# Layer 0 of a two-layer graph network: VectorE's one-hots of a counted quad are made one step ahead of TensorE's products of them

## The chip, the cores and the metric

The kernel runs on one core of a Trainium2 chip. The metric is the device time of one execution in microseconds (us), as the median of several runs. A profile of one execution gives the durations; its own time stands beside its span in the table below.

## The reference

3125 nodes with 128 features, 100,000 edges sorted by destination, two layers. Layer 0, with which this change deals, is a mean over neighbours, a linear map, an ELU and a layer norm:

```python
    msgs = x[edge_src]
    summed = jax.ops.segment_sum(msgs, edge_dst, num_segments=n_nodes)
    deg = jax.ops.segment_sum(jnp.ones_like(edge_dst, dtype=x.dtype), edge_dst, num_segments=n_nodes)
    mean_neigh = summed / jnp.maximum(deg, 1.0)[:, None]
    return jax.nn.elu(mean_neigh @ W + b)
    ...
    x = _layernorm(x + _L0_gnn_ref(x, src, dst, L0_gnn_W, L0_gnn_b), axis=-1)
    x = _layernorm(x + _L1_gnn_ref(x, edge_index, edge_attr_16, edge_type_4, ...), axis=-1)
```

Layer 1 is a relational attention with 4 relations and 4 heads over the same edges, a feed-forward part and layer norms. It gathers its rows from tables that layer 0's end writes to memory.

## The kernel before

**Tiles.** The edges lie in 784 tiles of 128; four tiles are a quad, so there are 196 quads. Because the edges are sorted, and their destinations crowd at the low nodes, the first 72 quads (`UD`) touch only few destinations each. The sums of layer 0 come about in two ways.

*Gathered quads* (72 to 195). GpSimd fetches the source rows of each tile with one indirect DMA (`gather`, L768), 24 tiles ahead. `sums0` (L1148) multiplies the rows with a one-hot of the destinations (4 tiles, one PSUM tile `sg`) and issues the gathers for the rows that come free. A step later ScalarE copies `sg` to SBUF (`out_copy`, L1158, `sgs`), VectorE makes another one-hot (`spread0`, L1162), and `out0` (L1166) issues six filler products into a part of PSUM that nobody reads (`fo<-ic,il`) and then the two products that spread the sums over 64 nodes (`fo<-ohq,sgs`). `add0` (L1176) adds `fo`, which has one buffer, to the accumulator on VectorE, at a place whose number is loaded into a register.

*Counted quads* (0 to 71). No row is fetched. `count` (L1197) makes for each of the quad's four tiles two one-hots in bf16 on VectorE: `ol` for the low seven bits of the source node, and `oc` for its block of 128 together with the destination. The product of the two, summed over the four tiles in the PSUM tile `dn`, counts how often each source meets each destination. `count_add` (L1209) adds these counts to the matrix `A` on VectorE, again at a loaded place. `ol` and `oc` have four buffers each, `dn` has one. The counted quads come in two segments, quads 0 to 51 and 52 to 71; at the end of each, `counted_sums` (L1223) multiplies `A` with the 25 blocks of `x` and adds the result to the accumulator. `dn` serves for this too.

**The steps.** A loop (L1360) over steps s handles the gathered quad 72 + s, and hangs other work onto it by a table `jobs`: a table of steps and kinds of work. Counted quads are put at steps 3 to 41 and 57 to 71, four to each three steps, so that 36 steps have one and 18 have two. Other jobs are the transposes and linear products of the edge attributes (`edges`, each fourth gathered quad of them all), the turning of attribute chunks, and the 25 node blocks: mean, norm, and a burst of table products (`tables`, L1313) whose results are cut into halves on VectorE a step later (`half`, L1328).

**What sets the order.** `Ordered` (L637) chains the instructions of TensorE, VectorE, ScalarE and SyncE in layer 0 in the order in which the Python code issues them, with no wait; GpSimd has such a chain for its gathers. So the order of the lines in the loop is the order on each engine: on TensorE transposes, the scatter of the last step's quad, linear products, counts, other jobs, row sums, burst; on VectorE halves, destination one-hot, spread one-hot, count one-hots, scatter's add, count's add, other jobs. In a step with two counted quads, the second quad's one-hots stand behind the first one's `count_add`:

```python
                for i, v in enumerate(counts):
                    count(v)
                    if i == 0 and UD < u <= NQ:
                        add0(u - 1)
                    count_add(v)
```

Of the kernel before, what the change touches and what calls it, by code (L numbers as in the profile page):

```python
# [9 lines left out]
F32 = mybir.dt.float32  # L10
I32 = mybir.dt.int32
U16 = mybir.dt.uint16
BF16 = mybir.dt.bfloat16
AF = mybir.ActivationFunctionType
OP = mybir.AluOpType
# [5 lines left out]
P = 128  # L21
N = 3125
E = 100000
F = 128
# [603 lines left out]
NQ = TT // 4  # L628
# [37 lines left out]
UD, ND, SHI = 72, 240, NB2  # L666
# [3 lines left out]
def counted(u):  # L670

    return 8 if u < 24 else 12 if u < SEG[0][1] else 16
# [20 lines left out]
def windows(ctx: ExitStack, tc: tile.TileContext, a, out, flag):  # L693
# [44 lines left out]
    def node(t, eng):  # L738
        return nc.values_load(d0_i[0:1, t:t + 1], engines=[eng], min_val=0, max_val=N - 1,
                              skip_runtime_bounds_check_because="a node's number")  # L740
# [16 lines left out]
    with tc.tile_pool(name="l0c", bufs=1) as l0c:  # L757
        acc0 = l0c.tile([P, 2, NPW], F32, name="acc0")

        XG, TD = 24, 4 * UD  # L760
# [3 lines left out]
        ic = l0c.tile([P, 16 * SHI], BF16, name="ic")  # L764
# [119 lines left out]
        with tc.tile_pool(name="m0c", bufs=1) as m0c, tc.tile_pool(name="l0", bufs=2) as l0, \  # L884
# [3 lines left out]
            pe, ve, act, sp = (Ordered(tc, e) for e in (nc.tensor, nc.vector, nc.scalar, nc.sync))  # L888
# [3 lines left out]
            def at_step(s, eng, f):  # L892
                jobs.setdefault((s, eng), []).append(f)
# [188 lines left out]
            def turned_at(f):  # L1082
                return 6 + f * (NS - 11) // (NQ // 4)
# [30 lines left out]
            X = {}  # L1114

            def onehot4(u):
                o = X["oh", u] = l0.tile([P, 4, WA], F32, name="oh", bufs=3)
                ve.tensor_tensor(o, loc_e[:, 4 * u:4 * u + 4].unsqueeze(2).to_broadcast([P, 4, WA]),
                                 iw[:, :WA].unsqueeze(1).to_broadcast([P, 4, WA]), op=OP.is_equal)
# [38 lines left out]
            def out_copy(u):  # L1158
                g = X["sgs", u] = l0.tile([P, F + 1], F32, name="sgs")
                act.activation(g, X.pop(("sg", u)), AF.Copy)  # L1160
# [5 lines left out]
            def out0(u):  # L1166
                g, q = X.pop(("sgs", u)), X.pop(("ohq", u))

                fb_ = l0p.tile([P, HC], F32, name="fo")
                for _ in range(6):  # L1170
                    pe.matmul(fb_[:, 2 * WQ:2 * WQ + 12 * SHI], il, ic[:, :12 * SHI], start=True, stop=True)
                fo = X["fo", u] = fb_[:, :2 * WQ].rearrange("p (a b) -> p a b", a=2)
                pe.matmul(fo[:, 0], g[:, :F], q, start=True, stop=True)
                pe.matmul(fo[:, 1], g[:, F:].to_broadcast([P, P]), q, start=True, stop=True)

            def add0(u):  # L1176
                n = node(4 * u, ENG.DVE)
                ve.tensor_tensor(acc0[:, :, ds(n, WQ)], acc0[:, :, ds(n, WQ)], X.pop(("fo", u)), op=OP.add)


            A = l0e.tile([P, SHI, ND + 16], F32, name="A")
            lo_f = l0e.tile([P, TD], F32, name="lo_f")
            c_f = l0e.tile([P, TD], F32, name="c_f")
            tmp_i = l0e.tile([P, TD], I32, name="tmp_i")

            def count_columns():
                ve.memset(A, 0.0)
                ve.tensor_scalar(tmp_i, src_e[:, :TD], P - 1, None, op0=OP.bitwise_and)
                ve.tensor_copy(lo_f, tmp_i)
                ve.tensor_scalar(tmp_i, src_e[:, :TD], 7, None, op0=OP.logical_shift_right)  # L1190
                ve.tensor_copy(c_f, tmp_i)
                for u0, u1 in ((0, 24), (24, SEG[0][1]), SEG[1]):
                    c = c_f[:, 4 * u0:4 * u1]
                    ve.tensor_scalar(c, c, float(counted(u0)), -200.0, op0=OP.mult, op1=OP.add)
                ve.tensor_add(c_f, c_f, loc_e[:, :TD])

            def count(u):  # L1197
                w = counted(u)
                cn = l0p.tile([P, SHI, w], F32, name="dn")
                for i in range(4):  # L1200
                    t = 4 * u + i
                    ol = l0.tile([P, P], BF16, name="ol", bufs=4)
                    ve.tensor_scalar(ol, il, lo_f[:, t:t + 1], None, op0=OP.is_equal)
                    oc = l0.tile([P, SHI * w], BF16, name="oc", bufs=4)
                    ve.tensor_scalar(oc, ic[:, :SHI * w], c_f[:, t:t + 1], None, op0=OP.is_equal)
                    pe.matmul(cn.rearrange("p a b -> p (a b)"), ol, oc, start=(i == 0), stop=(i == 3))
                X["cn", u] = cn

            def count_add(u):  # L1209
                n = nc.values_load(dc_i[0:1, u:u + 1], engines=[ENG.DVE], min_val=0, max_val=ND - 1,  # L1210
                                   skip_runtime_bounds_check_because="a node's number, bounded")
                v = A[:, :, ds(n, counted(u))]
                ve.tensor_tensor(v, v, X.pop(("cn", u)), op=OP.add)

            def x_block(b, s):
                n = min(P, N - b * P)
                xb = m0.tile([P, F], F32, name="xb", bufs=7)
                if n < P:
                    ve.memset(xb, 0.0)
                sp.dma_start(xb[:n], a["x"][b * P:b * P + n, :])  # L1220
                return xb

            def counted_sums(g, k):  # L1223
                if k == 0:
                    X["dn"] = l0p.tile([P, 2, ND], F32, name="dn")
                pe.matmul(X["dn"][:, 0], X.pop(("xc", k)), A[:, k, :ND], start=(k == 0), stop=False,
                          skip_group_check=True)
                if k == SHI - 2:
                    X["as"] = l0e.tile([P, ND], F32, name="as")
                    ve.tensor_reduce(X["as"], A[:, :, :ND].rearrange("p s n -> p n s"), AX.X, OP.add)  # L1230
                if k == SHI - 1:
                    pe.matmul(X["dn"][:, 1], ones, X.pop("as"), start=False, stop=True, skip_group_check=True)
                    n = 0 if g == 0 else nc.values_load(
                        dc_i[0:1, UD:], engines=[ENG.DVE], min_val=0, max_val=NP - ND,
                        skip_runtime_bounds_check_because="a node's number, bounded")
                    v = acc0[:, :, ds(n, ND)] if g else acc0[:, :, :ND]
                    ve.tensor_tensor(v, v, X.pop("dn"), op=OP.add)
# [118 lines left out]
            for f in range(NQ // 4):  # L1356
                at_step(turned_at(f), "edges", range(4 * f, 4 * f + 4))
            last = max(s for s, _ in jobs)
            onehot4(UD)
            for s in range(last + 1):  # L1360
                u = UD + s
                for f in jobs.pop((s, "sp"), []):
                    f()
                if UD < u <= NQ:
                    out_copy(u - 1)
                edges = jobs.pop((s, "edges"), [])
                for us in edges:
                    turned(us)
                halves_ = jobs.pop((s, "half"), [])
                if halves_:  # L1370
                    halves_.pop(0)()
                if u + 1 < NQ:
                    onehot4(u + 1)
                if halves_:
                    halves_.pop(0)()
                if u < NQ:
                    spread0(u)
                for f in halves_:
                    f()
                if UD < u <= NQ:  # L1380
                    out0(u - 1)
                for us in edges:
                    lin(us)
                counts = jobs.pop((s, "count"), [])
                for i, v in enumerate(counts):
                    count(v)
                    if i == 0 and UD < u <= NQ:
                        add0(u - 1)
                    count_add(v)
                if UD < u <= NQ and not counts:  # L1390
                    add0(u - 1)
                for us in edges:
                    lin_add(us)
                for e in ("act", "ve"):
                    for f in jobs.pop((s, e), []):
                        f()
                if u < NQ:
                    sums0(u)
                for f in jobs.pop((s, "burst"), []):
                    f()  # L1400
                for us in edges:
                    keep(us)
# [5 lines left out]
    with tc.tile_pool(name="ac", bufs=1) as ac, tc.tile_pool(name="at", bufs=2) as at, \  # L1408
# [93 lines left out]
        for j, (w, x, y) in enumerate((  # L1502
                (W, rF[0:1], rL[0:1]), (WQ - WW + 1, rF4[:, :, 0], rF4[:, :, 3]),
                (WW, rF4[:, :UQ, 0], rL4[:, :UQ, 3]), (WW, rF[0:1, 4 * UQ:4 * UP:2], rL[0:1, 4 * UQ + 1:4 * UP:2]))):
            n = x.shape[1]
# [3 lines left out]
        for u0, u1, j in ((0, 24, 8), (24, SEG[0][1], 9)):  # L1509
# [6 lines left out]
                                op0=OP.subtract, op1=OP.is_gt)  # L1516
# [30 lines left out]
        pe, ve, act, pool, sp = (Ordered(tc, e) for e in (nc.tensor, nc.vector, nc.scalar, nc.gpsimd, nc.sync))  # L1547
# [270 lines left out]
        for s in range(-2, NQ + LATE + 2):  # L1818
            u = s - 1
# [37 lines left out]
    with tc.tile_pool(name="fc", bufs=1) as fc, tc.tile_pool(name="fw", bufs=3) as fw, \  # L1857
# [89 lines left out]
        for bs_ in QS:  # L1947
            o = fw.tile([P, 4, F], F32, name="o")
            for i, b in enumerate(bs_):
                if b % 5 < 2:  # L1950
                    nc.scalar.activation(o[:, i], r1[:, b], AF.Identity, bias=nm[:, b:b + 1], scale=rs3[:, b:b + 1])
                else:
                    nc.vector.tensor_scalar(o[:, i], r1[:, b], mv3[:, b, 0:1], rs3[:, b:b + 1],
                                            op0=OP.subtract, op1=OP.mult)
            b = bs_[0]
            n = min(P, N - b * P)
# [27 lines left out]
```

## Time and profile before

| | |
|---|---|
| median of 3 runs | 2873.77 us (2867.88 to 2883.67) |
| profiled execution: its own time / its span | 2875.92 us / 2874.1 us |
| granted TensorE clock, mean of the span | 0.898 |
| busy: TensorE products, VectorE, GpSimd, ScalarE | 84%, 63%, 43%, 32% of the span |
| layer 0's loop | to about 1077 us |
| counted steps, first segment | 52.6 to 359.1 us, 39 steps |
| counted steps, second segment | 489.4 to 630.7 us, 15 steps |

In the profile a row of a group reads: source line (L647 is the line of the helper that issues all ordered instructions), engine, operation, out<-in by the tiles' names, shapes, count | busy us, mean ns of one | idle us of that engine just before them and what ended it. PE is TensorE's products, PEld its weight loads, DVE VectorE, ACT ScalarE, POOL GpSimd, SP SyncE. A row of the timeline has start, length, engine, instruction, and in brackets the idle time before it. A row of the waits reads "who waited <- for whom: us in total, times, longest". "Remote" is a semaphore whose update came from no instruction that the profile can name, and "issue" a wait for which it shows no cause. `dn<-oc,ol` are the counts' products, `A<-A,dn` is `count_add`, `fo<-ic,il` the fillers, `fo<-ohq,sgs` the scatter, `acc<-acc,fo` is `add0`, `sg<-xg,oh` the row sums, `xg` the gathers.

### The profile page before, as it was taken

The numbers are of one execution on the slowest core, as the hardware profiler recorded it, in microseconds if no ns is written. First come the engines' busy times: TensorE is split into PE (matmuls) and PEld (weight loads), VectorE is DVE, ScalarE is ACT, GpSimd is POOL, SyncE is SP. The second block draws the span as 40 slices with busy tenths as digits, with TensorE's granted clock in tenths as the row PEclk, the third lists the DMA queues.
The fourth block names the chain that finished last, engine by engine and source line by source line (L and its number), as shares of the span: only waits on it lengthen the run. The fifth ranks groups of instructions, "written<-read, shape, count | busy, mean of one in ns | idle before, by whom it ended". The sixth has DMA issues, their size and how long they took to land.

```text
span 2874.1 us, 66163 instructions
## 1 busy us (share of the span) xinstructions
PE 2417.7 (84%) x24485; PEld 1858.4 (65%) x24485; DVE 1821.4 (63%) x6395; ACT 908.9 (32%) x1964; POOL 1245.1 (43%) x1294
## 2 busy tenths in 40 slices
PE   3687777877777685699999999999999999999974
PEld 2454454445444443577777777888888888888853
DVE  6655535653544345377777777777777777776656
ACT  0121112212222231244444444444444443333314
POOL 6555443444434413244444444444444444444400
PEclk9757778878888787799999999999999999999977
DMA  4323344444455456466666667777777789999910
GB/s 128 90 73 104 112 137 142 138 125 155 147 186 173 139 197 227 128 210 205 205 205 208 205 205 216 235 236 235 236 235 233 235 241 245 254 243 246 236 53 24
DMA packets 284394, 520.64 MB, mean 181 GB/s; under 512 B 45833, under 2 KB 144820, under 8 KB 283151
## 3 DMA queue, kind: packets, MB, share of 16 engines
q1 hardware_dynamic: 201588, 273.76, 30.7%
q0 software_dynamic: 78592, 239.71, 29.6%
q8 instruction: 194, 3.18, 0.5%
q10 hardware_dynamic: 3880, 2.84, 0.4%
q14 instruction: 140, 1.15, 0.1%
HBM read 412.10 MB, written 104.82 MB: 180 GB/s over the span
## 4 chain that ended last, share of the span: by engine, by line
PE 48%; DVE 8%; issue 3%; DMA 2%; ACT 0%; SPq 0%; DVEq 0%; ACTq 0%
PE z L647 30%; PE ag L647 7%; PE row L647 6%; DVE wo L647 4%; PE e L647 2%; PE sm_p L647 2%; DMA win<-xr_d 1%; DVE f L647 0%; DVE oh L647 0%; DVE ea L647 0%; PE f L1930 0%; PE f L1922 0%; DVE acc L647 0%; DMA xr_d<-xh 0%; DVE fst L1886 0%
## 5 line engine op out<-in xcount | busy, mean ns | idle before, releaser
L647 POOL DMA_INDIRECT xl<-xl_d,src_e x784 | 751.5, 959 | 895.8 <-PE ag L647 391.5
L647 POOL DMA_INDIRECT xg<-in_x_dram,src_e x496 | 489.0, 986 | 542.6 <-PE sg L647 368.5
L647 ACT ACTIVATE relu<-z 128x512 f32<-128x512 f32 x784 | 449.1, 597 | 793.7 <-PE z L647 611.1
L647 PE MATMUL z<-f_ident,xl 128*128 128x128 f32 x3136 | 476.1, 274 | 0.0
L647 PEld LDWEIGHTS z<-f_ident,xl 128*128 128x128 f32 x3136 | 368.7, 141 | 44.3 <-issue 0.6
L647 PE MATMUL z<-ea,weh 128*128 128x512 f32 x784 | 360.9, 460 | 18.4 <-issue 14.1
L647 PE MATMUL z<-oht,win 96*128 96x128 f32 (+2 forms) x1600 | 343.4, 297 | 4.1 <-DMA win<-xr_d 2.2
L647 PEld LDWEIGHTS z<-oht,win 128*128 128x128 f32 (+1 forms) x1600 | 275.4, 190 | 60.6 <-issue 3.2
L647 PE MATMUL z<-ea,wel 128*128 128x512 f32 x784 | 310.1, 395 | 0.1
L647 PE MATMUL row<-relu,attw 128*32 128x128 f32 x6272 | 247.7, 277 | 31.1 <-issue 29.4
L647 PE MATMUL ag<-xl,wo 128*32 128x128 f32 x6272 | 225.6, 279 | 7.5 <-DVE acc L647 4.2
L647 PEld LDWEIGHTS row<-relu,attw 128*32 128x32 f32 x6272 | 172.6, 109 | 85.0 <-issue 84.0
L647 PE MATMUL xp<-cbl,two 128*128 128x512 f32 x200 | 165.4, 827 | 30.5 <-DVE xh L647 13.1
L647 DVE TENSOR_TENSOR acc<-acc,fo 128x128 f32 x124 | 35.3, 285 | 245.0 <-remote 97.9
L647 PEld LDWEIGHTS ag<-xl,wo 128*32 128x32 f32 x6272 | 181.1, 112 | 9.1 <-DVE acc L647 5.1
L647 DVE TENSOR_TENSOR_SCAN m<-rm,row 128x128 f32<-128x128 bf16 x98 | 41.2, 420 | 228.4 <-PE row L647 228.4
L647 PE MATMUL fo<-ic,il 128*128 128x300 bf16 x744 | 153.5, 357 | 37.4 <-DVE acc L647 31.3
L647 DVE CAST xh<-xp 128x512 fp32r<-128x512 f32 x100 | 69.0, 690 | 157.3 <-PE xp L647 113.7
L647 PEld LDWEIGHTS z<-ea,weh 128*128 128x128 f32 x784 | 149.5, 191 | 27.5 <-issue 27.5
L647 ACT ACTIVATE xlr<-xp 128x512 f32<-128x512 f32 x100 | 59.7, 597 | 304.3 <-PE xp L647 156.2
L647 PEld LDWEIGHTS z<-ea,wel 128*128 128x128 f32 x784 | 150.1, 191 | 9.0 <-issue 0.4
L647 DVE SCALAR_TENSOR_TENSOR ea<-far,e 128x512 fp32r<-128x512 bf16 x196 | 132.2, 675 | 36.7 <-remote 35.6
(327 smaller groups left out, 4059.3 us busy)
## 6 DMA issues: line engine op xcount, KB each, us to landing
win<-xr_d SPq DMA_DIRECT2D x224, 256.0 KB
xr_d<-xh SPq DMA_DIRECT2D x100, 512.0 KB
win<-xr_d SPq DMA_DIRECT2D x176, 192.0 KB
xl_d<-xlr SPq DMA_DIRECT2D x100, 258.0 KB
sg<-seg_d SPq DMA_DIRECT2D x196, 128.0 KB
rm<-rq_d SPq DMA_DIRECT2D x98, 128.5 KB
eat_d<-emt SPq DMA_DIRECT2D x196, 64.0 KB
xl<-xl_d,src_e POOLq DMA_INDIRECT x784
```

Of the source, the lines that this page charges most:

```text
L647: ins = f(*args, **kw)
```

## The change

`count` is split. It now only makes the one-hots of a quad and keeps them; `count_out` issues their four products, and `count_add` is as before. `ol` and `oc` get eight buffers each. In the loop, the one-hots made in a step are kept in `made`, and their products come in the next step: the first quad's at its head, ahead of `out_copy` and of the transposes and the scatter; its `count_add` behind the halves and the spread one-hot on VectorE; a second quad's products behind the scatter; the new one-hots behind these; then `add0`; then the second quad's `count_add`. To make room, the integer work tile of `count_columns` becomes a view of `A`, which is cleared after it; `as`, a sum over `A`, takes a buffer of the table rows `xlr`; and the blocks of `x` get six buffers for seven.

```diff
-            tmp_i = l0e.tile([P, TD], I32, name="tmp_i")
+            tmp_i = A.rearrange("p s n -> p (s n)")[:, :TD].bitcast(I32)
...
             def count(u):
-                w = counted(u)
-                cn = l0p.tile([P, SHI, w], F32, name="dn")
+
+                n = SHI * counted(u)
                 for i in range(4):
                     t = 4 * u + i
-                    ol = l0.tile([P, P], BF16, name="ol", bufs=4)
+                    ol = l0.tile([P, P], BF16, name="ol", bufs=8)
                     ve.tensor_scalar(ol, il, lo_f[:, t:t + 1], None, op0=OP.is_equal)
-                    oc = l0.tile([P, SHI * w], BF16, name="oc", bufs=4)
-                    ve.tensor_scalar(oc, ic[:, :SHI * w], c_f[:, t:t + 1], None, op0=OP.is_equal)
+                    oc = l0.tile([P, n], BF16, name="oc", bufs=8)
+                    ve.tensor_scalar(oc, ic[:, :n], c_f[:, t:t + 1], None, op0=OP.is_equal)
+                    X["oc", t] = ol, oc
+
+            def count_out(u):
+                cn = X["cn", u] = l0p.tile([P, SHI, counted(u)], F32, name="dn")
+                for i in range(4):
+                    ol, oc = X.pop(("oc", 4 * u + i))
                     pe.matmul(cn.rearrange("p a b -> p (a b)"), ol, oc, start=(i == 0), stop=(i == 3))
-                X["cn", u] = cn
...
-                xb = m0.tile([P, F], F32, name="xb", bufs=7)
+                xb = m0.tile([P, F], F32, name="xb", bufs=6)
...
-                    X["as"] = l0e.tile([P, ND], F32, name="as")
+                    X["as"] = m0.tile([P, ND], F32, name="xlr", bufs=3)
...
+            made = []
             onehot4(UD)
             for s in range(last + 1):
                 u = UD + s
                 for f in jobs.pop((s, "sp"), []):
                     f()
+                if made:
+                    count_out(made[0])
                 if UD < u <= NQ:
                     out_copy(u - 1)
...
+                for v in made[:1]:
+                    count_add(v)
                 if UD < u <= NQ:
                     out0(u - 1)
+                for v in made[1:]:
+                    count_out(v)
                 for us in edges:
                     lin(us)
                 counts = jobs.pop((s, "count"), [])
-                for i, v in enumerate(counts):
+                for v in counts:
                     count(v)
-                    if i == 0 and UD < u <= NQ:
-                        add0(u - 1)
+                if UD < u <= NQ:
+                    add0(u - 1)
+                for v in made[1:]:
                     count_add(v)
-                if UD < u <= NQ and not counts:
-                    add0(u - 1)
+                made = counts
```

More of the change, by code (lines that the diff above doesn't have):

```diff
@@ L1183, in windows @@
             c_f = l0e.tile([P, TD], F32, name="c_f")
-            tmp_i = l0e.tile([P, TD], I32, name="tmp_i")
+            tmp_i = A.rearrange("p s n -> p (s n)")[:, :TD].bitcast(I32)
             def count_columns():
-                ve.memset(A, 0.0)
                 ve.tensor_scalar(tmp_i, src_e[:, :TD], P - 1, None, op0=OP.bitwise_and)
@@ L1191, in count_columns @@
                 ve.tensor_copy(c_f, tmp_i)
+                ve.memset(A, 0.0)
                 for u0, u1 in ((0, 24), (24, SEG[0][1]), SEG[1]):
```

## The prediction, on record before the result was known

> **What bounds the kernel now.** I first read the page's slices and its chain, then the busy times by stretch, then the groups by shape, the waits, and last the timeline of one step. The chain that ended last begins only with layer 0's last tables (its first long piece is a table product at 1104 us), so it doesn't show what paces the counted steps. They must be judged in their own stretches: 88 to 359 us (quads 0 to 51, after a start held up by weight loads) and 489 to 631 us (quads 52 to 71).
>
> ```profile
> PEclk9757778878888787799999999999999999999977
> ```
> ```profile
> 88.00:359.00 271.00, 211.84 (x1141) 131.71 (x1141) 163.93 (x686) 43.17 (x101) 137.93 (x143) 0.69 0.33 95
> 489.00:631.00 142.00, 112.91 (x563) 65.61 (x562) 90.25 (x322) 31.07 (x76) 54.95 (x57) 0.82 0.42 144
> ```
>
> The columns are stretch, length, busy PE, PEld, DVE, ACT, POOL, granted clock, DMA share, GB/s. TensorE is busy 78% and 80% of the time, VectorE 60% and 64%, nobody is full, and TensorE runs at 0.69 and 0.82 of its clock. Two in-order engines pass work to and fro. Where TensorE loses time to it:
>
> ```profile
> L647 PE MATMUL dn<-oc,ol 128*128 128x300 bf16 x112 | 30.8, 356 | 17.5 <-remote 5.6 <-DVE ol L647 3.3 <-DVE oc L647 3.2
> L647 PE MATMUL dn<-oc,ol 128*128 128x200 bf16 x96 | 24.8, 324 | 14.0 <-DVE oc L647 6.4 <-issue 2.8 <-DVE xlr L647 2.6
> L647 PE MATMUL dn<-oc,ol 128*128 128x400 bf16 x80 | 24.8, 380 | 10.3 <-DVE oc L647 5.3 <-DVE ol L647 2.2 <-issue 1.5
> ```
>
> These are the counts' products; the figure behind the second bar is TensorE's idle time just ahead of them: 17.5 + 14.0 + 10.3 = 41.8 us. One step with two counted quads shows the mechanism, TensorE first, then VectorE:
>
> ```profile
> 132.41 0.51 PE L647 MATMUL dn<-oc,ol 128*128 128x200 bf16 x4
> 134.99 1.35 PE L647 MATMUL dn<-oc,ol 128*128 128x200 bf16 x4 [2.07 <-DVE oc L647]
> 136.27 0.66 PE L647 MATMUL sg<-xg,oh 128*32 128x129 f32 x8
> 136.86 1.68 PE L647 MATMUL fo<-ic,il 128*128 128x300 bf16 x6
> 138.33 0.95 PE L647 MATMUL fo<-ohq,sgs 128*128 128x64 f32 x4
> ```
> ```profile
> 131.72 0.29 DVE L647 TENSOR_TENSOR acc<-acc,fo 128x128 f32 x1 [1.16 <-issue]
> 134.22 0.36 DVE L647 TENSOR_TENSOR A<-A,dn 128x200 f32 x1 [2.22 <-PE dn L647]
> 134.50 0.25 DVE L647 TENSOR_SCALAR ol<-il,lo_f 128x128 bf16<-128x128 bf16 x1
> ```
>
> VectorE had made the first quad's one-hots by 130.6 and then stood, first for the scatter's sum, then for the counts (its add started 1.3 us after the last product's recorded end, 132.92). Only then could it make the second quad's one-hots, and TensorE stood 2.07 us. Gathers aren't the limit: they follow at 1.25 us (218.52, 219.77, 221.03 in GpSimd's timeline), so 5.0 us for a step's four, while 54 counted steps take 448 us from 52.6 to 359.1 and 489.4 to 630.7, 8.3 each. GpSimd waits for TensorE.
>
> ```profile
> POOL xg L647 <- PE sg L647: 92.9, 28, 14.4
> DVE A L647 <- PE dn L647: 25.5, 26, 3.3
> ```
>
> [...] with a grant of 0.50 from 107.0 to 124.1 us[...]: that stretch was busy 16.10 of 17.10 us. [...] the second quad's one-hots, which need no product's result, start behind the waiting add. [...] another such add started 0.42 us after its product. That spread is the main uncertainty below.
>
> **The change, part by part.** The sum is made against the profiled execution's own 2875.92 us (span 2874.1); the median of the runs is 2873.77, 2.1 less.
>
> 1. *The one-hots move a step ahead.* 72 quads keep 8 one-hots, 4 products and one add each; nothing is added to or taken from any engine. A step now begins on TensorE with the first quad's four products, whose one-hots are finished. The second quad's products follow the scatter's products, and by then the first add has freed their bank: behind the first products TensorE has 6 filler and 4 scatter products (1.68 + 0.95, about 2.4 us at half clock), against 0.4 to 1.3 us of hand-over and 0.36 to 0.57 us of add. So the 41.8 us go, but for two terms: 2.5 us lie at 83 us, in the start that waits for weights and can't gain; and the 5.6 us "remote" is a product's semaphore that came late, which may strike elsewhere, so I count half of it. Removed: 41.8 - 2.5 - 2.8 = 36.5 us (bounds 30 and 39.3).
>
> 2. *The clock.* A clock of 0.69 means half speed for (1 - 0.69) / 0.5 = 62% of the stretch; 212 us busy are then 212 / 1.62 = 131 us of full-speed work. If closing the gaps cuts the slow share by a fifth (to 50%), that saves 131 x 0.12 = 16 us; in the second stretch (36% to 29%, 113 / 1.36 = 83 us) another 6. Half of these 22 us will lie beside other waits: 11 us gained. Nothing in the trace shows a step after the change, so the bounds are wide: 35 gained if the slow share nearly halves, 10 lost[...].
>
> 3. *What the moved waits hold up.* On VectorE the first count's add now stands ahead of the next step's one-hots, and the scatter's add behind all of these; the next step's filler products wait for the scatter's add, since `fo` has one buffer. The way from the head's products to that add: hand-over 0.4, add 0.4, four pairs of one-hots 1.5 us (129.05 to 130.56; 3.0 where two quads are made), scatter's add 0.3, hand-over 0.2: 2.8 or 4.3 us. Beside it TensorE has, in a bare step at half clock, filler and scatter 2.4, row sums 0.6, next head 1.1: 4.1 us; at full clock half of it, 2.1. So it is short by 0.2 us in double steps at half clock, by 0.7 and 2.2 us at full clock. With full clock in some 45% of the 54 steps: 36 x 0.45 x 0.7 + 18 x (0.45 x 2.2 + 0.55 x 0.2) = 11 + 20 = 31 us as the upper bound. Transposes, linear products and tables lengthen the cover in many steps, and a bare step at full clock meets the 5.0 us of its gathers anyway; lower bound 0. I take 13 us lost.
>
> 4. *The rest.* `tmp_i` in A's place and the later memset: same instructions at step 1, before the weights hold everything; nothing. `as` in the ring of `xlr`: asked for at steps 54 and 84, whose last table rows left four and more steps before, and freed a step later; nothing. `xb` with 6 for 7 buffers: two are loaded and two used per step on SyncE's queue, a step ahead, so 4 live; nothing, or a wait of SyncE that TensorE doesn't see. GpSimd's queue keeps its order: its gathers come when row sums free their rows, sooner if TensorE is sooner. One step less lies between the last count and the blocks' sums; the add stands ahead of them on VectorE, so about 1 us twice at worst, within the rounding.
>
> Sum: -36.5 - 11 + 13 = -34.5 us: 2875.9 - 34.5 = 2841.4 profiled, less 2.1: **2839 us** as a median. Layer 1 starts when layer 0's last tables are out, by order and not by the clock, so the whole passes through to the end.
>
> **Rivals.** *The stall only moves (0.23).* The scatter's add becomes the late one: all 31 us of step 3, no gain of clock: 2873.8 - 36.5 + 31 = 2868 us. For it speaks "PE fo <- DVE acc", with 6.7 us already waited in the first stretch; against it, that these are 3 waits only, two of them behind late semaphores. *More than I think (0.14).* The clock comes free and step 3 is covered: -39.3 - 35 = -74, 2799 us; for it speaks that half the TensorE time there is at half speed, against it the 16.10 of 17.10 us that didn't release it. *Slower (0.13).* VectorE's early wait for the step's head is the mechanism: a hand-over of 1.3 us as at 134.22, not 0.4, now stands ahead of one-hots and scatter's add in each of the 54 steps. At two thirds of them exposed, 36 x 0.9 = 32 us, with the 31 of step 3 and a clock 5 lost to the idling: 2873.8 - 36.5 + 31 + 32 + 5 = 2905 us. It decides from 36.5 / 54 = 0.7 us per counted step put on TensorE's path. That the change doesn't do what it says is unlikely: buffers for 8 tiles hold just the two quads of a step.
>
> **Chances.** The forecast's own case has 0.50 (about 2820 to 2858). A measurement of this kernel can tell about 0.5%, 14.4 us, from no change. Faster by more: 0.50 + 0.14 = 0.64; within: 0.23; slower: 0.13. The range goes from the best case, 2799, to 2885, the sum of the bad bounds (-30 + 10 + 31 = +11); outside lie most of the slow case and a tail of the fast one.
>
> **What would show it.** Right: idle ahead of `dn<-oc,ol` under 8 us (now 41.8), "DVE A <- PE dn" still there, clock from 88 to the end of the first counts above 0.69, counted steps at about 7.6 us. Step 3 wrong: "PE fo <- DVE acc" above 20 us in counted steps. The prediction is wrong if TensorE's idle time there stays at its 59 + 29 = 88 us in the two stretches under other names, or if time is lost after 631 us, which no step of mine explains.

## The result, and the profile after

The changed kernel takes **2839.97 us** (median of 4 runs, 2831.36 to 2846.67), the kernel before beside it 2870.82: a ratio of 0.9895, 95% interval 0.9856 to 0.9933, or 31 us. The forecast was 2839. The sum came out; its terms didn't, as the profile of the changed kernel shows. Its profiled execution took 2831.36 us (span 2829.6), the shortest of the four.

The page's row of granted clocks, and the stretches that hold the same work before and after. The scatter's sum `acc` serves as a mile post: the counted steps lie between its 5th and 42nd execution, 37 steps, and between its 57th and 72nd, 15 steps. Columns as in the prediction (length, then busy PE, PEld, DVE, ACT, POOL, clock). First the kernel before:

```profile
86.50:368.00 281.50, 216.45 (x1170) 134.84 (x1169) 165.73 (x696) 44.20 (x103) 143.49 (x148) 0.69 0.33 94
498.20:632.40 134.20, 105.32 (x538) 62.09 (x537) 83.88 (x306) 27.36 (x67) 55.91 (x58) 0.81 0.40 134
```

Then the changed one:

```profile
PEclk8677788887788887899999999999999999999967
```
```profile
82.20:354.50 272.30, 191.30 (x1173) 132.31 (x1172) 166.51 (x696) 44.22 (x102) 140.01 (x146) 0.74 0.33 97
489.30:608.90 119.60, 91.42 (x522) 57.66 (x521) 82.05 (x299) 25.93 (x64) 57.92 (x60) 0.87 0.45 146
```

The two stretches together shrink from 415.7 to 391.9 us, 24 us. TensorE's *busy* time falls by 39 us (321.8 to 282.7) with the same products; its *idle* time, which the change was to remove, rises by 15 us (93.9 to 109.2). By the end of layer 0's loop (the start of the last `acc`, 1077.1 and 1045.7 us) the changed kernel is 31 us ahead.

The groups of the counts' products, changed kernel (behind the bar: busy, mean ns, idle just ahead):

```profile
L647 PE MATMUL dn<-oc,ol 128*128 128x300 bf16 x112 | 27.5, 371 | 7.1 <-DVE A L647 3.8 <-PE sg L647 2.2 <-issue 0.5
...
L647 PE MATMUL dn<-oc,ol 128*128 128x400 bf16 x80 | 20.9, 371 | 7.5 <-DVE A L647 2.9 <-PE sg L647 2.6 <-issue 1.1
...
L647 PE MATMUL dn<-oc,ol 128*128 128x200 bf16 x96 | 18.3, 317 | 11.4 <-DVE A L647 6.0 <-issue 3.5 <-DVE ol L647 1.4
```

The idle time here fell from 41.8 to 26.0 us. One-hots are named only once among the first three causes, with 1.4 us; what is named first is `A`, the add that frees the one bank of `dn`. New idle time came up elsewhere. Here is the scatter in the whole program, before and after:

```profile
L647 PE MATMUL fo<-ohq,sgs 128*128 128x64 f32 x496 | 94.5, 326 | 68.3 <-issue 49.2 <-ACT sgs L647 19.1
```
```profile
L647 PE MATMUL fo<-ohq,sgs 128*128 128x64 f32 x496 | 92.1, 320 | 91.0 <-issue 62.7 <-ACT sgs L647 28.3
```

In the two stretches alone it is 10.2 and then 31.9 us, and ahead of `mw<-vt,emt`, products of the edge attributes, 10.1 and then 17.8. Both read what ScalarE copies, though for most of this time the trace names no cause ("issue"). And ScalarE waits like this (waits of the changed kernel: us in total, times, longest):

```profile
ACT sgs L647 <- remote: 152.2, 29, 11.4
...
DVE acc L647 <- remote: 43.8, 8, 11.9
...
DVE A L647 <- remote: 14.0, 5, 5.9
```

One such event, ScalarE first, then TensorE:

```profile
116.60 0.28 ACT L647 ACTIVATE sgs<-sg 128x129 f32<-128x129 f32 x1 [10.03 <-remote]
```
```profile
109.05 0.66 PE L647 MATMUL sg<-xg,oh 128*32 128x129 f32 x8
...
110.67 0.93 PE L647 MATMUL fo<-ic,il 128*128 128x300 bf16 x6
116.93 1.09 PE L647 MATMUL fo<-ohq,sgs 128*128 128x64 f32 x4 [5.33 <-issue]
```

The row sums ended at 109.7 us; ScalarE copied them at 116.6, with nothing else to do, and TensorE stood 5.3 us for the copy. I call a hand-over late if its consumer, being idle, starts over 2 us after the recorded end of the products that it needs. Counted for `acc`, `sgs` and `A`, the kernel before has 42 late ones, 183 us in all, the changed one 52, 235 us. That could be the change's doing or the chip's; runs on other chips are set beside it below.

### The profile page after: what moved, and what is told of

The parts are those of the page before. It is cut to its first block, busy times and chain, and to the rows that moved or that the text cites. A ratio compares the mean times of both kernels' runs of the same rounds, so it can differ in the third digit from the quotient of the medians.

```text
span 2829.6 us, 66188 instructions
## 1 busy us (share of the span) xinstructions
PE 2375.0 (84%) x24485; PEld 1850.4 (65%) x24485; DVE 1822.5 (64%) x6395; ACT 909.4 (32%) x1964; POOL 1240.3 (44%) x1294
## 4 chain that ended last, share of the span: by engine, by line
PE 49%; DVE 8%; issue 3%; DMA 1%; ACT 0%; DVEq 0%; SPq 0%; ACTq 0%
PE z L647 30%; PE ag L647 7%; PE row L647 6%; DVE wo L647 4%; PE e L647 2%; PE sm_p L647 2%; DVE f L647 1%; DMA win<-xr_d 1%; DVE ea L647 0%; DVE oh L647 0%; PE f L1942 0%; PE f L1934 0%; DVE y L647 0%; DVE de L647 0%; DVE m L647 0%
## 5 line engine op out<-in xcount | busy, mean ns | idle before, releaser
L647 PEld LDWEIGHTS z<-f_ident,xl 128*128 128x128 f32 x3136 | 368.1, 141 | 44.3 <-issue 0.6
L647 PE MATMUL fo<-ohq,sgs 128*128 128x64 f32 x496 | 92.1, 320 | 91.0 <-issue 62.7
L647 PE MATMUL fo<-ic,il 128*128 128x300 bf16 x744 | 143.9, 341 | 27.3 <-issue 18.3
L647 PEld LDWEIGHTS fo<-ohq,sgs 128*128 128x128 f32 x496 | 85.5, 240 | 112.3 <-issue 70.9
```

The lines of the kernel that those rows point to most:

```text
L647: ins = f(*args, **kw)
```

## The experiments

Mile posts are used throughout: "stretches" are the two above, with 37 and 15 steps. The first four kernels ran on one chip, where the kernel before took 2868.15 us (40 runs). "The first chip" stands for this one and for the result above, which has the same time before (2870.82) and the same late hand-overs.

**The changed kernel again** (e1)

> The changed kernel once more. If its profile is typical: about 2840 us, ratio 0.989, TensorE's idle time ahead of the counts' products near 20 us (42 before) and some 25 us more than before ahead of the scatter's products, behind ScalarE's copy. If the first profile was a lucky one, layer 1 (from the last scatter's sum to the end), which was 13 us shorter there, comes back to 1797 us as in the kernel before, and the loop of layer 0 keeps its 31 us.

Measured: 2843.29 us, ratio 0.9917 (0.9891 to 0.9944). Stretches 388.0 us, busy 279.5, idle 108.5: the same signs as above, less busy and more idle than before. Idle time ahead of the counts' products is 32.7 us, where I expected near 20; ahead of the scatter's it is 27 us more than before, as expected. The loop ends 25.8 us ahead. Layer 1 took 1794 us, before 1797, and 1784 in the first profile. Those 13 us are no part of the change: e3 below, which gains nothing, has 1784 too.

**The buffers alone** (e2): the kernel before with the room changes and eight buffers, in the old order.

```diff
-                    ol = l0.tile([P, P], BF16, name="ol", bufs=4)
+                    ol = l0.tile([P, P], BF16, name="ol", bufs=8)
```

> The kernel before with all that makes room (work tile in A, the sum in the table rows' ring, six blocks of x) and with eight buffers of each one-hot, but the old order of the step. Theory (what counts is where the one-hots stand in VectorE's order): no gain, 2868 to 2874 us, idle ahead of the counts' products still about 42 us. Rival (buffers or the moved tiles bring it): about 2840 us.

Measured: 2862.87 us, 0.9984 (0.9958 to 1.0009). Buffers and room bring nothing that can be told from zero.

**All one-hots first, in the same step** (e3): two quads' one-hots and the scatter's sum ahead of both quads' products, no step of lead.

```diff
+                for v in counts:
+                    count(v)
+                if UD < u <= NQ:
+                    add0(u - 1)
+                for v in counts:
+                    count_out(v)
+                    count_add(v)
```

> Eight buffers, no lead: in a step all its one-hots are made first, then the scatter's add, then products and add of the first quad, then of the second. So only the round trip in the 18 steps with two quads goes. Theory (the lead counts): half of the gain or less, 2853 to 2865 us, with TensorE still waiting for one-hots of the same step. Rival (only the one-hots behind the add were the stall): the whole gain, about 2840 us.

Measured: 2863.56 us, 0.9995 (0.9977 to 1.0013). Idle time ahead of `dn<-oc,ol` is 50.5 us (20.0 + 12.5 + 18.0), of which 27.4 us are named `A`: the second quad waits for its bank where it waited for one-hots. TensorE's busy time in the stretches falls by 20 us (321.8 to 302.1), and its idle time rises by 17.5 (93.9 to 111.4).

**The lead, with the products in their old place** (e4): one-hots a step ahead, but the products stand behind scatter and linear products, and on VectorE the scatter's sum and the first add stand ahead of the one-hots.

```diff
-                if made:
-                    count_out(made[0])
...
+                for v in made[:1]:
+                    count_out(v)
...
+                for v in made[:1]:
+                    count_add(v)
+                for v in made[1:]:
+                    count_out(v)
+                for v in counts:
+                    count(v)
```

> One-hots a step ahead as in the changed kernel, but the products stay where they were, behind the scatter and the linear products, and on VectorE both adds come ahead of the new one-hots. Theory (the lead counts, not the place at the step's head): within 8 us of the changed kernel, 2832 to 2848 us. Rival (the gain comes from products at the head, which fill TensorE's wait for ScalarE's copy of the row sums): most of it goes, 2855 us or more.

Measured: 2878.74 us, 1.0030 (1.0011 to 1.0049), slower. My theory, that the lead is what counts and its place doesn't, fell here. But this kernel changes two things at once, the place on TensorE and the order on VectorE, so the next two kernels look at each.

The next four ran on a second chip. There the kernel before takes 2552.17 us, 11% less, and in none of these four traces does any hand-over to `acc`, `sgs` or `A` come over 2 us late.

**The sum ahead of the one-hots** (e5): the changed kernel, one thing altered.

```diff
-                for v in counts:
-                    count(v)
                 if UD < u <= NQ:
                     add0(u - 1)
+                for v in counts:
+                    count(v)
```

> The changed kernel with one thing altered: VectorE makes the scatter's sum (acc) ahead of the one-hots of the next step, not behind them; the products keep their new places (first quad at TensorE's head of a step, second behind the scatter's products). Four cells are compared with this one: head/behind (the changed kernel, 2843), head/ahead (this), old place/ahead (2879, measured), old place/behind. If the place of the products carries the gain, this one is 2840 to 2850 us, and a few us faster than the changed kernel if step 3 of the prediction (the scatter's sum held up by the one-hots) is real. If VectorE's order carries it (one-hots ahead of every wait for a product), this one loses most of the gain: 2860 to 2880 us, with idle time ahead of dn<-oc,ol back above 30 us.

**Both products in the old place** (e6): one-hots a step ahead and ahead of the sum, the products behind scatter and linear products, both adds of the counts last on VectorE. So the first add moves too, which it must: its products come later.

```diff
-                if made:
-                    count_out(made[0])
...
-                for v in made[1:]:
+                for v in made:
+                    count_out(v)
                     count_add(v)
```

> The fourth cell: one-hots a step ahead and on VectorE ahead of the scatter's sum, as in the changed kernel, but both counted quads' products stand on TensorE behind the scatter's products and the linear products, as before the change, and VectorE makes both adds of the counts last. If the place at the step's head carries the gain (TensorE has finished work at hand while ScalarE copies the row sums), this one loses it: 2865 to 2885 us, as the run with the old place and the adds first. If VectorE's order carries it, this one keeps it: 2838 to 2850 us.

Measured: e5 2530.06 us, 0.9918 (0.9894 to 0.9942), the ratio that I had expected if the place carries the gain, but with 47.4 us of idle time ahead of the counts' products, which I had expected if VectorE's order does; e6 2572.01 us, 1.0076 (1.0050 to 1.0102). What the four cells mean is told below, with the changed kernel's run on such a chip.

**The scatter a step further behind** (e7, on the changed kernel; e8, on the kernel before): takes away what TensorE waits for when it waits for `sgs` of the same step.

```diff
-                if UD < u <= NQ:
-                    out0(u - 1)
+                if UD + 1 < u <= NQ:
+                    out0(u - 2)
```

> The changed kernel, and the scatter's products and their sum a further step behind (the row sums of quad u are copied by ScalarE in step u+1 as now, and used in step u+2; the last two quads are caught up in one step; three buffers of ohq for two; blocks that are not the last start a step later). TensorE then never waits for the copy sgs of the same step. If the changed kernel's remaining idle time (27.5 us ahead of fo<-ohq,sgs in the first stretch) is ScalarE's wait and its late hand-overs, it is faster than the changed kernel by 10 to 35 us: 2808 to 2833. If that idle time only takes another name (the sum's slot, gathers, the wait for emt), it stays within 2838 to 2850.

> The kernel before with the same lag of the scatter's products, no one-hot ahead. If the old order's loss is the one-hots' own (TensorE stands until they are made), the lag helps both kernels alike or the old one less: 2845 to 2870, and 20 us or more above the changed kernel with the lag. If the changed kernel's gain is that its products fill the time of ScalarE's copy, the lag takes that time away for both, and this one comes within 10 us of the changed kernel with the lag.

Measured: e7 2511.45 us, 0.9841 (0.9813 to 0.9868); e8 2570.46 us, 1.0066 (1.0030 to 1.0102). With the old order the lag gains nothing in the stretches (349.8 us; e12 below has 345.0) and loses behind the last count (338.5 us; e12 has 323.2). The two kernels with the lag are 59 us apart, not within 10. So on this chip the wait for ScalarE's copy isn't what the change is worth. There was little of it to win: on calm chips TensorE's idle time ahead of the scatter's products is 0.4 us in the stretches of the kernel before and none in the changed one. On the first chip, where it is 10.2 and 31.9 us, the lag wasn't tried, so the forecast for e7 wasn't tested where it was made.

The last four ran on a third chip, as calm as the second: 2553.38 us before, no late hand-over.

**The two kernels on a calm chip** (e11 the changed one, e12 the one before)

> The changed kernel once more, beside the kernel before on one chip. The last four kernels ran on a chip on which the kernel before takes 2552 us, not 2870, and on which no product's semaphore came over 2 us late (on the first chip some 190 to 240 us of such late hand-overs per run). If the gain doesn't rest on the late hand-overs, the ratio is 0.990 to 0.994 on either chip (2527 to 2537, or 2842 to 2853). If the change only hides part of them, the ratio is above 0.997 on the calm chip. With the sum ahead of the one-hots at 0.9918, step 3 of the prediction (13 us) would put this one at 0.997.

> The kernel before, for its profile on this chip: the stretch of counted steps (scatter sums 4 to 41) to set beside the others. On the calm chip, 207 us with the place at the head, 237 with the old place and the one-hots a step ahead, 233 with the old order and the lag. If the head's place carries the gain, the kernel before takes 225 to 235 us there, with the clock near 0.76; and idle time ahead of dn<-oc,ol of 30 us or more.

Measured: changed 2504.20 us, ratio **0.9800** (0.9765 to 0.9836), a gain of 49 us where the first chip gave 25 to 31. I expected 0.990 to 0.994 or less of a gain; it is more. So late hand-overs aren't what the change hides. Where they occur the gain is about half as large; which of TensorE's waits make the difference is told further below. The kernel before came out as expected (first stretch 233.2 us at a clock of 0.75, 44.7 us idle ahead of the counts). Before, then changed (stretches, and the counts' groups):

```profile
65.90:299.10 233.20, 196.09 (x1167) 124.35 (x1166) 165.81 (x695) 44.56 (x103) 152.09 (x158) 0.75 0.39 116
395.70:507.50 111.80, 91.90 (x539) 54.82 (x538) 83.75 (x307) 27.47 (x67) 55.01 (x57) 0.92 0.48 160
```
```profile
64.20:256.60 192.40, 162.74 (x1159) 115.48 (x1159) 163.18 (x696) 44.09 (x102) 146.39 (x152) 0.85 0.46 139
353.40:455.60 102.20, 87.59 (x525) 56.43 (x524) 81.27 (x299) 26.48 (x64) 55.24 (x58) 0.92 0.50 168
```
```profile
L647 PE MATMUL dn<-oc,ol 128*128 128x300 bf16 x112 | 29.6, 329 | 14.9 <-DVE oc L647 11.2 <-DVE ol L647 0.7
...
L647 PE MATMUL dn<-oc,ol 128*128 128x200 bf16 x96 | 24.4, 314 | 17.6 <-DVE oc L647 13.6 <-DVE ol L647 2.1 <-DVE acc L647 0.2
L647 PE MATMUL dn<-oc,ol 128*128 128x400 bf16 x80 | 23.9, 364 | 12.2 <-DVE oc L647 10.7
```
```profile
L647 PE MATMUL dn<-oc,ol 128*128 128x300 bf16 x112 | 25.8, 343 | 3.5 <-DVE A L647 1.8 <-DVE ol L647 0.8 <-DVE oc L647 0.2
...
L647 PE MATMUL dn<-oc,ol 128*128 128x400 bf16 x80 | 19.4, 345 | 6.0 <-DVE oc L647 2.8 <-DVE A L647 2.6
...
L647 PE MATMUL dn<-oc,ol 128*128 128x200 bf16 x96 | 15.5, 264 | 10.2 <-DVE oc L647 4.7 <-DVE ol L647 2.2 <-DVE A L647 2.0
```

Here the account is clean. The stretches shrink by 50.4 us (345.0 to 294.6), as much as the whole gain. TensorE's busy time falls by 37.7 (288.0 to 250.3), the same as on the first chip (39.1, and 42.3 in the repeat); its idle time falls by 12.7 (57.0 to 44.3), where it rose by 15 on the first chip. Ahead of the counts 25.0 us of idle time go in the whole program (44.7 to 19.7), 21.7 of them in the stretches (40.9 to 19.2); there 9.8 us come back as the wait for the scatter's sum, "PE fo <- DVE acc" (none before, 6.4 and 3.4 in the two stretches now). In TensorE's account the chips differ in the idle term and hardly in the busy one. VectorE is busy for 244 of the 295 us, 83%, more than before (250 of 345, 72%).

The four cells (products' place, and the scatter's sum against the next step's one-hots on VectorE), with the stretches together; the kernel before has 1 and 345.0 us:

| | one-hots ahead of the sum | sum ahead of the one-hots |
|---|---|---|
| first products at the step's head | 0.9800, 294.6 us (the change) | 0.9918, 320.9 us (e5) |
| products behind scatter and linear products | 1.0076, 364.1 us (e6) | 1.0030 (e4, first chip) |

Three cells are on the two calm chips, whose times before agree to 0.05%; the fourth is on the first chip, so its ratio isn't strictly comparable. The head's place, with the early add that it allows, is needed: without it, neither order that was tried gains. With it, the order on VectorE is worth another 26 us of the stretches. In e6 TensorE waits for the sum and for the bank:

```profile
PE fo L647 <- DVE acc L647: 37.4, 24, 7.6
...
PE dn L647 <- DVE A L647: 33.0, 18, 2.5
```

The same double step in the changed kernel and in e5 shows what VectorE's order does. VectorE of the changed kernel, then of e5:

```profile
139.13 0.34 DVE L647 TENSOR_TENSOR A<-A,dn 128x200 f32 x1
139.41 0.24 DVE L647 TENSOR_SCALAR ol<-il,lo_f 128x128 bf16<-128x128 bf16 x1
...
142.38 0.27 DVE L647 TENSOR_TENSOR acc<-acc,fo 128x128 f32 x1
...
143.96 0.47 DVE L647 TENSOR_TENSOR A<-A,dn 128x300 f32 x1
```
```profile
151.33 0.34 DVE L647 TENSOR_TENSOR A<-A,dn 128x200 f32 x1
151.87 0.29 DVE L647 TENSOR_TENSOR acc<-acc,fo 128x128 f32 x1 [0.20 <-PE fo L647]
152.08 0.25 DVE L647 TENSOR_SCALAR ol<-il,lo_f 128x128 bf16<-128x128 bf16 x1
...
156.66 0.47 DVE L647 TENSOR_TENSOR A<-A,dn 128x300 f32 x1
```

In the changed kernel VectorE makes one-hots while TensorE scatters, and the sum finds its products long done. In e5 it stands 0.20 us for the scatter, the one-hots start later, and the next add, which frees the bank for the second quad, comes 5.33 us after the last one, not 4.83. TensorE then stands 1.57 us ahead of the second quad's products, against 0.46; the changed kernel pays 0.95 us of that back ahead of the fillers, where it waits for the sum. One pair of steps proves little, since the difference goes from -2.5 to +3.5 us over the 52 steps. The counts' groups of e5 show it for all of them:

```profile
L647 PE MATMUL dn<-oc,ol 128*128 128x300 bf16 x112 | 25.9, 320 | 16.1 <-DVE A L647 9.4 <-DVE oc L647 3.0 <-DVE ol L647 1.6
L647 PE MATMUL dn<-oc,ol 128*128 128x400 bf16 x80 | 21.9, 371 | 12.3 <-DVE A L647 6.9 <-DVE oc L647 4.7
L647 PE MATMUL dn<-oc,ol 128*128 128x200 bf16 x96 | 17.7, 278 | 19.0 <-DVE A L647 10.9 <-DVE oc L647 6.0 <-DVE ol L647 0.9
```

The wait for `A` is 27.2 us, against 6.4 in the changed kernel. In the stretches e5 stands 26.3 us longer ahead of the counts' products (45.5 for 19.2) and 9.8 us less for the sum; other idle time adds 5.0 us and busy time 4.8.

**The lag only in the counted steps** (e9): e7 was 20 us slower than e5 behind the last count (339.4 to 319.2), so here the lag ends there, and between the segments.

```diff
+            def late(s):
+                return int(s <= 43 or 58 <= s <= 72)
...
+                todo = [v for v in range(UD, min(u, NQ)) if v > done and v < u - late(s)]
```

> The changed kernel with the scatter's products a further step behind only in the steps with counts (0 to 43 and 58 to 72), caught up in the step after. In the run with the lag everywhere, the counted steps went at 5.0 us (185.1 us for 37, the gathers' pace), 22 us below the run without the lag, but the steps after the last count were 20 us longer (339.4 for 319.2). If the loss there comes of the lag in those steps, this one keeps both: 20 us below the lag everywhere, ratio 0.974 to 0.979. If it comes of the earlier start of the later steps (clock or tables due at the same time), the ratio stays at 0.982 to 0.986.

Measured: 2506.56 us, 0.9794 (0.9755 to 0.9834), the same as the changed kernel, and neither of the two outcomes in full. The later part is indeed as without the lag (319.4 us), but the counted steps did not keep what e7 had there (287.4 us in the stretches): they take 297.9, the changed kernel 294.6. No version that I tried beats the change beyond its interval.

**Fillers in the old gap** (e10): is it the clock?

```diff
+                    if i == 0:
+                        for _ in range(3):
+                            pe.matmul(cn.rearrange("p a b -> p (a b)"), il, ic[:, :SHI * w], start=True, stop=True)
```

> The kernel before with three filler products (il by ic, of the counts' own size, into the counts' bank, overwritten by the counts) ahead of each quad's products, where TensorE stands until the one-hots are made; nothing computed is altered. If the gain of the change is mostly TensorE's clock[...], this one gains too: ratio 0.990 to 0.997, with the clock in the counted steps up by 0.08 or more. If the gain is the products' own place (work at hand in ScalarE's time), the fillers only delay: ratio 0.999 to 1.008.

Measured: 2541.38 us, 0.9949 (0.9928 to 0.9970), faster by 12 us. The stretches:

```profile
65.90:288.80 222.90, 190.01 (x1312) 126.61 (x1311) 166.21 (x698) 44.51 (x103) 150.84 (x157) 0.87 0.41 120
383.70:498.10 114.40, 98.31 (x599) 59.00 (x598) 83.71 (x306) 27.45 (x67) 54.16 (x56) 0.97 0.46 155
```

216 useless products, 41.4 us busy (16.0 + 13.4 + 12.0 in their groups), lie in TensorE's queue, and the program is faster: the clock rises from 0.75 to 0.87 and from 0.92 to 0.97, and TensorE's busy time, fillers included, stays at 288.3 us (288.0 without), so all other products took some 41 us less. The stretches shrink by 7.7 us, all of it idle time (57.0 to 49.0). So the clock is a lever by itself. The change gets less clock and more gain: it pays for no fillers, and its products need 250.3 us.

## Why the prediction was right in sum and wrong in its terms

| step, in the stretches | predicted | calm chip | first chip |
|---|---|---|---|
| 1, idle ahead of the counts | -36.5 | -21.7 | -18.1 |
| 2, TensorE's busy time (clock) | -11 | -37.7 | -39.1 |
| 3, idle ahead of the fillers (the sum) | +13 | +9.8 | -1.0 |
| not in the sum: idle ahead of `fo<-ohq,sgs` and `mw<-vt,emt` | 0 | -0.4 | +29.4 |
| all other idle time | 0 | -0.4 | +5.0 |
| sum | -34.5 | -50.4 | -23.8 |
| median, whole | -35 | -49 | -31; repeat -25 |

On the first chip 8 us more of the loop's gain came outside the stretches.

**Step 1, too large.** "So the 41.8 us go, but for two terms" failed at "by then the first add has freed their bank". On the first chip 12.7 of the 26.0 us that are left in the whole program are named `A`, on the calm one 6.4 of 19.7. There 10.7 are still named one-hots: VectorE makes eight pairs for a double step, and its timeline above runs from 139.13 to past 142.38 without a wait. The forecast "under 8 us" was wrong on either chip.

**Step 2, too small by a factor of three.** That closing gaps raises the clock, and idling lowers it, was an assumption of mine, as were the 35, 10 and 5 us that I put on it; no trace of the kernel before showed it. The sign was right: with the change the granted clock rose from 0.69 to 0.74 and from 0.81 to 0.87 on the first chip, from 0.75 to 0.85 on the calm one (there 0.92 in the second stretch, before and after), and in e10 filled gaps alone raised it (0.75 to 0.87). The term was mis-sized, in two places. The slow share of the first stretch fell by two fifths on the calm chip ((1 - 0.75) / 0.5 = 50% to 30%), not by a fifth. And "half of these 22 us will lie beside other waits" was wrong there: beside the 37.7 us, idle time elsewhere rose by no more than step 3 had put down for itself.

Not all of the 37.7 us are clock. The traces show a granted clock of 0.5 or of 1.0 and nothing between (on the first chip 55 records of each in the kernel before, 49 of each in the changed one), so the products can be sorted by what was granted when each began, each counted with the busy time that it adds to those before it. In the first stretch of the calm pair a counts' product at half clock takes 262 ns before and 263 after; at full clock it takes 221 before (110 products) and 158 after (151). In the second stretch it is 250 (65) and 217 (72) at full clock. Other products at full clock in the first stretch hardly change (119 and 117 ns). So at full clock four products whose one-hots come one by one are drawn out, and the short waits between them count as busy. The other kernels agree: 197 ns in e10, where one-hots still come one by one, 117 and 121 in e4 and e6, where they lie ready. As an estimate that is 63 ns for 110 to 151 products and 33 ns for 65 to 72, 9 to 12 us; the other 26 to 29 go with the clock. I had put the drawn-out products nowhere.

**Step 3, about right on a calm chip.** The wait for the scatter's sum went from nothing to 9.8 us in the counted steps, for 13 forecast, and stays under the 20 that I had named as refuting it. On the first chip it fell, in the whole program from 31.3 to 6.4 us (23.7 in the repeat), while late hand-overs strike `A` and `sgs` more often (11 late ones at `A`, 1 before). What I had not seen is that this wait is the cheaper side: e5 takes it away and loses 26 us. That half of step 3, VectorE's adds waiting behind TensorE, was priced; its remedy would have cost more.

**Step 4, right.** Buffers and room: 0.9984 (0.9958 to 1.0009).

**The signs.** Counted steps took 391.9 / 52 = 7.5 us (7.6 forecast), and the clock rose (0.69 to 0.74 in the first stretch). But by my own test, "wrong if TensorE's idle time stays at its 88 us under other names", the argument is refuted on the first chip: the idle time is 109 us there, against 94 before in the same stretches. The test was a poor one, because it left my own step 2 out: busy time moves as well. The time came out by luck, through errors that cancel. On the first chip TensorE's idle time was to fall by 23.5 us (steps 1 and 3) and rose by 15; its busy time was to fall by 11 and fell by 39. The idle term itself holds two errors: on a calm chip it falls by 12.7, so that some 11 us are my overrating of the stall, and some 28 are the first chip's, for which I had no term. They have a place: ahead of `fo<-ohq,sgs` and `mw<-vt,emt`, which wait for ScalarE's copies, idle time rose by 29.4 us there (20.3 to 49.7; 50.0 in the repeat) and on the calm chip not at all. That the late hand-overs to ScalarE make this wait is what the event at 116.60 shows once; for the whole of it I infer it.

**Of the rivals,** "the stall only moves" holds for the first chip's idle time and not for the time; "more than I think" comes closest to the calm chip's 49 us, by the clock, as it said; "slower" named VectorE's early wait for the head's products. On the calm chip that fell, from 39.5 to 9.1 us ("DVE A <- PE dn"); on the first chip it is real: VectorE stood 51.8 us in the 11 late hand-overs to `A`, with one-hots and sum behind it, where one of 3.3 us stood before.

What stays open: why the first chip hands over late; how the change would do there with a lag for `sgs`; and how much of the loss of e6 is the products' place and how much the late add that goes with it.

## What to carry to other kernels

Where filled gaps come with more clock, as on TensorE here (0.75 to 0.87 in e10), read busy time as a quantity that the change moves, with its own row in the sum; compare it over the same work. Put work that is finished early at the head of a step of the engine that waits, and make it, on the other engine, ahead of an instruction that waits for this step's products: in this kernel either alone brought at most half of the gain. And before trusting a stall's size, see whether it comes back on another chip.

## What the hardware showed that I had not expected

**Late hand-overs came with one chip of three.** The kernel before takes 2868 us on one chip and 2552 and 2553 on two others, an eighth more for the same program. On the first, consumers of TensorE's products start over 2 us late 42 times in layer 0 (183 us in all, the longest 11.8); on the others never, and no wait there is put down to "remote". 246 of the 326 us between the spans are lost by the end of layer 0's loop (1077.1 and 830.6 us). The late ones take 4.4 us in the mean (183 / 42), a hundred times the usual 0.04 us (the median delay of `acc`). TensorE's own stalls beside them, as the 5.33 us at 116.93 above, show that the time is real.

Where the delay arises can be narrowed. In 40 of the 42 cases TensorE's semaphore has a recorded update within 0.15 us ahead of the late start, so the time passes before that update and not after it. But the first chip's traces are also poorer: the one of the kernel before holds 3484 of VectorE's 5675 semaphore updates and 3999 of TensorE's 4632, on the calm chip 5632 and 4574. So the names of releasers there, "remote" above all, are less sure. Whether the product or its semaphore is late, and whether the recording itself has a part in the delay, no run here tells.

**Filling a gap with useless products paid** (e10): with 41.4 us of them the granted clock went from 0.75 to 0.87 and from 0.92 to 0.97, and the program took 12 us less.
